# Softmax sums from the exponential's accumulator instead of from products, and the ends of query tiles begun two steps earlier

## The chip, the cores and the metric

The kernel runs on one core of a Trainium2 chip, in one launch. Its engines work beside each other, each on its own queue of instructions: TensorE multiplies matrices (the profile has a row for its products, PE, and one for its weight loads, PEld), VectorE (DVE), ScalarE (ACT) and GpSimd (POOL) do the element-wise work, and SyncE (SP) issues most of the DMAs. The metric is the device time of one execution in microseconds; several runs of a kernel are compared by their medians.

## The reference

Four blocks follow each other on `x` of shape 4 x 512 x 128, all in fp32, each `x = layernorm(x + block(x))`. The change touches the first and, through its order, the second.

```python
# block 1: attention with relative positions, 8 heads of 16
score   = (einsum('bqhd,bkhd->bhqk', q + u_bias, k) + rel_shift(einsum('bqhd,khd->bhqk', q + v_bias, p))) / sqrt(e)
attn    = softmax(score, axis=-1)
ctx     = einsum('bhqk,bkhd->bqhd', attn, v).reshape(b, s, e)
return ctx @ Wo + bo
# block 2: each token goes to one of 8 experts (its largest gate), F = 512
h  = silu(xn @ W1[e] + b1[e]);  ye = h @ W2[e] + b2[e];  out = ye[top1] * top1_score
# block 3: in-projection, causal convolution of 3, gates a, b, c, and the recurrence over 512 positions
state = a_t * state + b_t * u_t;  y_t = c_t * state + u_t
# block 4: each token goes to one of 14 experts, F = 256, gelu
```

## The kernel before

**Attention** is 64 steps (`steps`, L1320): a batch b of 4, a tile t of 128 queries of 4, and a pair p of heads of 4. The loop `attention` (L1331) writes the instructions of each engine out in order, by hand. Step k issues:

- the turning (`flip`, L986) of the probabilities of step k-2: four TensorE transposes of 128x128 into a PSUM bank `ptr`, and a ScalarE copy to `prT`, once before and once after the scores;
- `scores` (L938) of step k: TensorE products into the PSUM tiles `main` and `aux`;
- in every second step `values` (L997), for the two pairs of step k-4 and k-3: 16 products of `prT` with V into `ctx`, and a ScalarE copy into `cT`. V has a column of ones beside each head's 16 columns (L878 to L880), so that `ctx` holds each head's sum of probabilities too;
- `softmax` (L968) of step k: two predicated copies and the row maximum (`nmax`) on VectorE, and one ScalarE exponential of 128x512 per head, into `pr`. The probabilities are not normalized here.

**Side work** goes between these steps: generators in the list `side`, each of which is advanced a little per step. They prepare later batches (`attn_prep`), finish query tiles and batches (`tiles_end`, `attn_end`), route tokens to experts (`route`, `dispatch`), and run the first half of the experts of block 2 (`experts(0, 0, ...)`, batches 0 and 1). All of it shares two PSUM banks (`any`) with `ptr` and `ctx`. A step therefore has a fixed number of places, `room[0]` (L1358): two products' groups of side work, or one if the step also issues a `ctx`. A generator that finds no place left waits for the next step (`bank`, L410). `pause(n)` lets n steps go by.

**The end of a query-tile pair**, `tiles_end` (L1009), runs eight times, for two tiles of one batch each. It takes one place for `pn`: 16 products of 128x4 against `sel` that pick the sums out of `cT`. VectorE inverts them (`rec`), and spreads them (`wide`). A second place goes to `prr` (four transposes of `wide`), after which VectorE multiplies `cT` by it; a third to `po`, the product with the output weights, which VectorE adds to the residual `xs`. The generator is put into `side` when the last `ctx` of its pair has been issued, three steps after the pair's last exponential (L1366). After the second pair of a batch, `attn_end` (L1049) follows: layer norm into `xf`, the transposed `xfT`, then `route` (L523) with its gate product `pl` and the counts of tokens per expert, and `dispatch` (L602) with the product `rank`, which gives every token its place in the sorted rows, and the scatters. Batches are dispatched in two groups, 0 and 1, then 2 and 3 (`GROUPS`). The second batch of a group goes on from the first one's counts.

**After attention**, `play` (L376) interleaves generators by a modelled clock (`Clock`, L63): it takes the first one whose needs are ready at the modelled time, and one that yields `BLOCKED` is passed over for that round. `rest_of_last` (L1641) brings the last query-tile pair (L1647), the last batch's end and routing, and then the experts of batches 2 and 3 (`experts(1, 0, ...)`, whose tokens are transposed into `pxs`). `rest_of_first` (L1631) brings what the first experts have left: up-products `ph`, down-products `py`. Wherever the model expects TensorE to wait more than 2 us for a PSUM bank's first product, it puts products of 128x512 in front whose result nobody reads (`pass_time`, L97, issued at L1666); they are called passes here.

All other instructions are issued by one helper, so that the profile shows them all at its line, L193; they are told apart by tile names.

Of the kernel before, what the change touches and what calls it, by code (L numbers as in the profile page):

```python
# [198 lines left out]
def tile_kernel(ctx: ExitStack, tc: tile.TileContext, x, wpack, cols, rows, tabs, b2bd0, b2bd1,  # L199
# [168 lines left out]
    def done():  # L368

        return clock.last  # L370
# [33 lines left out]
    def pause(n):  # L404

        if now[0] is not None:
            for _ in range(2 * n):
                yield

    def bank(*needs):  # L410
        if psum_e is not None:
            yield (*needs, common_bank)
            return
        while now[0] is not None and not room[0]:
            yield
            yield
        room[0] -= 1
# [101 lines left out]
        return ap.unsqueeze(2).to_broadcast([P, NT, n_e])  # L519

    chosen, before, shares, slots, extra = {}, {}, {}, {}, {}

    def route(xT, weights, n_e, b, layer, out):  # L523

        nm = f"{layer}_{b}"
        gr = GROUP[b]
        at = GROUPS[gr].index(b) * NT
        if at == 0:
            n_t = len(GROUPS[gr]) * NT
            chosen[layer, gr] = plan.tile([P, n_t, n_e], F32, tag=f"chosen{layer}_{gr}", name=f"chosen{nm}")  # L530

            before[layer, gr] = plan.tile([P, n_t + 1, n_e], F32, tag=f"before{layer}_{gr}", name=f"before{nm}")
            nc.gpsimd.memset(before[layer, gr][:, 0, :], 0.0)
        mine = chosen[layer, gr][:, at : at + NT, :]
        w = small.tile([P, NT, 32], F32, tag="w", bufs=5, name=f"w{nm}")
        out.append(w)
        nc.gpsimd.memset(w, 0.0)
        yield from bank(xT)
        lg = ps(f"pl{nm}")[:, : NT * n_e].rearrange("p (n e) -> p n e", e=n_e)
        for n in range(NT):  # L540
            nc.tensor.matmul(lg[:, n, :], lhsT=xT[:, n * P : (n + 1) * P], rhs=weights, start=True, stop=True)
        yield (done(),)
        mx = small.tile([P, NT], F32, tag="mx", name=f"mx{nm}")
        nc.vector.tensor_reduce(mx, lg, AX.X, ALU.max)
        eq = small.tile([P, NT, n_e], F32, tag=f"eq{n_e}", name=f"eq{nm}")
        nc.vector.tensor_tensor(eq, lg, over(mx, n_e), ALU.is_equal)
        ex = small.tile([P, NT, n_e], F32, tag=f"ex{n_e}", name=f"ex{nm}")
        nc.vector.tensor_tensor(ex, lg, over(mx, n_e), ALU.subtract)
        if layer == 0:
            nc.scalar.activation(ex, ex, AF.Exp)  # L550
        else:

            nc.scalar.activation(ex, ex, AF.Tanh, scale=0.5)
        nc.vector.tensor_tensor(eq, eq, ramps[n_e].unsqueeze(1).to_broadcast([P, NT, n_e]), ALU.mult)
        first = small.tile([P, NT], F32, tag="first", name=f"first{nm}")
        nc.vector.tensor_reduce(first, eq, AX.X, ALU.max)
        nc.vector.tensor_tensor(mine, eq, over(first, n_e), ALU.is_equal)
        so_far = before[layer, gr]
        for n in range(at, at + NT):
            nc.vector.tensor_tensor(so_far[:, n + 1, :], so_far[:, n, :], chosen[layer, gr][:, n, :], ALU.add)  # L560
        yield
        yield from pause(1)

        def weighted():
            if layer == 1:
                den = small.tile([P, NT, n_e], F32, tag=f"den{n_e}", name=f"den{nm}")
                nc.vector.tensor_scalar(den, ex, -1.0, 1.0, ALU.mult, ALU.add)
                nc.vector.reciprocal(den, den)
                nc.vector.scalar_tensor_tensor(ex, ex, 1.0, den, ALU.add, ALU.mult)
            sm = small.tile([P, NT], F32, tag="sm", name=f"sm{nm}")  # L570
            nc.vector.tensor_reduce(sm, ex, AX.X, ALU.add)
            share = keep.tile([P, NT], F32, tag=f"share{layer}", name=f"share{nm}")
            nc.vector.reciprocal(share, sm)
            shares[layer, b] = share
            nc.vector.tensor_tensor(w[:, :, :n_e], mine, over(share, n_e), ALU.mult)

        yield from dispatch(b, (xf_of if layer == 0 else x3)[b], n_e, (F0, F1)[layer], ("b1_0", "b1_1")[layer], layer,
                            weighted)
        yield
# [22 lines left out]
    def dispatch(b, its_rows, n_e, n_f, b1, layer, meanwhile):  # L602
# [12 lines left out]
        nov = NOV[gr]  # L615
        mine = slice(i * NT, (i + 1) * NT)
        eq, cum = chosen[layer, gr], before[layer, gr]
        yield from bank(cum, eq)
        both = ps(f"rank{nm}")
        flat, pc = both[:, : NT * n_e], both[:, NT * n_e : (NT + 1) * n_e]  # L620
# [347 lines left out]
    def softmax(b, t, p, main, aux):  # L968

        nm = f"{b}_{t}_{p}"  # L970
        c0 = t * P
        wd = min(P, S - c0 - 1)
        nc.vector.copy_predicated(main[:, :, c0 : c0 + P], low.bitcast(U32).unsqueeze(1).to_broadcast([P, 2, P]),
                                  aux[:, :, 0, :])
        nc.vector.copy_predicated(main[:, :, c0 + 1 : c0 + 1 + wd],
                                  ident[:, :wd].bitcast(U32).unsqueeze(1).to_broadcast([P, 2, wd]), aux[:, :, 1, :wd])
        nmax = small.tile([P, 2], F32, tag="nmax", name=f"nmax{nm}")
        nc.vector.tensor_reduce(nmax, main, AX.X, ALU.max, negate=True)
        prs = []
        for i in range(2):  # L980
            pr = ap6.tile([P, S], F32, tag="pr", name=f"pr{nm}_{i}")
            nc.scalar.activation(pr, main[:, i, :], AF.Exp, bias=nmax[:, i : i + 1])
            prs.append(pr)
        return prs

# [6 lines left out]
        nc.scalar.copy(prT.rearrange("p c q -> p (c q)"), ptr)  # L992
        return prT

    cTs = {}

    def values(b, t, g, prTs):  # L997

# [10 lines left out]
    def tiles_end(b, t2):  # L1009

        nm = f"{b}_{t2}"
        cT = cTs.pop((b, t2))
        yield from bank(cT)
        pn = ps(f"pn{nm}")[:, : 2 * NG * 4]
        for i in range(2):
            for g in range(NG):
                at = (i * NG + g) * 4
                nc.tensor.matmul(pn[:, at : at + 4], lhsT=cT[:, i, g, :], rhs=sel, start=True, stop=True)
        yield (done(),)
        rec = small.tile([P, 2 * NG * 4], F32, tag="rec", bufs=1, name=f"rec{nm}")  # L1020
        nc.vector.reciprocal(rec, pn)
        wide = ap2.tile([P, 2 * NG, 4, 2 * DH], F32, tag="wide", bufs=1, name=f"wide{nm}")
        nc.vector.tensor_copy(wide.rearrange("p g h d -> p (g h) d"), rec.unsqueeze(2).to_broadcast([P, 2 * NG * 4, 2 * DH]))
        yield
        yield from bank(wide)
        pr_ = ps(f"prr{nm}")
        for g in range(2 * NG):
            nc.tensor.transpose(pr_[:, g * P : (g + 1) * P], wide[:, g].rearrange("p h d -> p (h d)"), ident)
        yield (done(),)
        flat = cT.rearrange("p i g q -> p (i g q)")  # L1030
        nc.vector.tensor_tensor(flat, pr_, flat, ALU.mult)
        yield
        yield from bank(cT)
        po = ps(f"po{nm}")
        for i in range(2):
            for g in range(NG):
                nc.tensor.matmul(po[:, i * D : (i + 1) * D], lhsT=cT[:, i, g, :], rhs=wwo[:, g, :],
                                 start=(g == 0), stop=(g == NG - 1))
        yield (done(),)
        mine = xs[b][:, 2 * t2 : 2 * t2 + 2, :].rearrange("p n d -> p (n d)")  # L1040
        nc.vector.tensor_tensor(mine, po[:, : 2 * D], mine, ALU.add)
        if t2 == 1 and b < B - 1:
            gen = attn_end(b)
            side.insert(0, gen)
            if b == GROUPS[0][-1]:
                urgent.append(gen)
        yield
# [283 lines left out]
    def attention(first, last):  # L1331

        for k in range(first, last):
# [29 lines left out]
            for gen in halves:  # L1363
                if gen in side and next(gen, "end") == "end":
                    side.remove(gen)
            if due is not None and due[2] == 1 and due[1] % 2 == 1:  # L1366
                side.insert(int(side[:1] == urgent), tiles_end(due[0], due[1] // 2))

    def wide_ps(name):
        if psum_e is None:  # L1370
# [273 lines left out]
    def rest_of_last():  # L1644
        last_experts = experts(1, 0, pack[0], E0, F0, "b1_0", col("rms_w"))
        next(last_experts)
        yield from tiles_end(B - 1, 1)  # L1647
        yield from attn_end(B - 1)
        yield from last_experts
        load_layer1()  # L1650
        while 1 not in gxs:
            yield BLOCKED
        backs = []
        for b in GROUPS[1]:
            yield (made[0, 1], lambda: clock.free["gpsimd"])
            backs.append(gather(b, 0))
        for b, back in zip(GROUPS[1], backs):
            yield from layer0_end(b, back)
        for b in GROUPS[1]:
            while b - 2 not in over_with:  # L1660
                yield BLOCKED
            begin(recurrence(b), -1)
        yield from layer1(1)
# [114 lines left out]
```

## Time and profile before

| | |
|---|---|
| runs | 579.96, 582.27, 586.38 us; median 582.27 |
| the profiled execution's own time | 601.35 us |
| its span, from first to last instruction | 599.4 us |
| mean granted TensorE clock | 0.888 |
| preparation, before the steps of attention | 0 to 17 us |
| attention with its side work | 17 to 331 us; TensorE busy 280.5, ScalarE 171.0, VectorE 204.3 |
| the last batch's way to its experts | 331 to 374 us; TensorE busy 35.6 |
| second half of block 2's experts | 374 to 410 us; TensorE busy 31.8 of 36 |
| block 3, the recurrences | 410 to 497 us; TensorE busy 82.6 of 87 |
| block 4 | 497 to 599.4 us; TensorE busy 67.3 |

The profile shows one execution, which took 3% longer than the median of the runs. Durations in it are those of that execution. In a row of groups the columns are the line, the engine and the operation, the tile written and the tiles read, the number of instructions, their busy time in us and the mean of one in ns, and behind the bar the idle time of the engine just before them and what ended most of it. In the rows of tenths each digit is a fortieth of the span; PEclk is the clock that was granted to TensorE, as a share of full speed: 9 is full, 5 is half.

### The profile page before, as it was taken

The page shows a single profiled execution, that of the slowest core. Times are in us where ns is not written, and L with a number is a line of the kernel's source. Part 1 is how long each engine was busy: PE and PEld are TensorE (multiplying, and loading weights), DVE is VectorE, ACT ScalarE, POOL GpSimd, SP SyncE. Part 2 cuts the span into 40 slices and gives each one's busy share as a digit, 9 for nine tenths or more (in the row PEclk, how much of TensorE's full clock was granted, in tenths as well). Part 3 has the DMA queues.
Part 4 walks back from the last instruction along what each step waited for, and adds up shares of the span by engine and source line. Part 5 has one row for each costly group of instructions (what it writes and reads, how often), then busy time and mean ns, then how long its engine had stood idle before and what let it go on. Part 6 is the DMA issues. An engine that isn't in the chain of part 4 may idle for free.

```text
span 599.4 us, 11301 instructions
## 1 busy us (share of the span) xinstructions
PE 512.4 (85%) x4132; PEld 362.6 (60%) x4132; DVE 374.4 (62%) x1033; ACT 293.3 (49%) x619; POOL 168.0 (28%) x272
## 2 busy tenths in 40 slices
PE   8988999979689898889898896899989988888740
PEld 6455665756446675567777693796455445876730
DVE  3786776755556746567766664596686689661415
ACT  1256565663546543456665130255546445655541
POOL 2482150230610400202200242522731304143324
PEclk9999999985879957579999787899979979998785
DMA  8998550410000560200118634862100006247321
GB/s 308 333 325 234 135 98 19 82 45 1 19 1 2 89 211 1 72 15 1 71 38 282 212 104 146 302 194 66 35 1 1 18 1 170 85 117 205 104 74 57
DMA packets 63847, 64.03 MB, mean 107 GB/s; under 512 B 4784, under 2 KB 53296, under 8 KB 63536
## 3 DMA queue, kind: packets, MB, share of 16 engines
q1 hardware_dynamic: 61744, 59.12, 33.3%
q0 software_dynamic: 2048, 4.20, 2.2%
q8 instruction: 32, 0.52, 0.4%
q14 instruction: 23, 0.19, 0.1%
HBM read 44.16 MB, written 20.45 MB: 108 GB/s over the span
## 4 chain that ended last, share of the span: by engine, by line
PE 60%; DVE 20%; issue 7%; ACT 6%; DMA 3%; POOL 2%; SPq 0%; DVEq 0%; ACTq 0%; POOLq 0%
PE ptr L193 9%; PE main L193 7%; PE py L193 7%; PE pa L193 6%; PE ph L193 6%; DVE nmax L193 6%; PE ctx L193 5%; DVE main L193 5%; PE aux L193 4%; PE pj L193 3%; DVE hb L193 2%; ACT pr L193 2%; PE pqa L193 1%; PE pxs L193 1%; PE pl L193 1%
## 5 line engine op out<-in xcount | busy, mean ns | idle before, releaser
L193 PE MATMUL ptr<-ident,pr 128*128 128x128 f32 x512 | 91.0, 306 | 22.0 <-ACT prT L193 6.2
L193 ACT COPY prT<-ptr 128x512 f32<-128x512 f32 x128 | 74.5, 587 | 65.3 <-PE ptr L193 63.6
L193 ACT ACTIVATE pr<-main,nmax 128x512 f32<-128x512 f32 x128 | 81.3, 687 | 49.0 <-DVE nmax L193 46.2
L193 PEld LDWEIGHTS ptr<-ident,pr 128*128 128x128 f32 x512 | 61.3, 153 | 66.0 <-issue 15.6
L193 DVE TENSOR_REDUCE nmax<-main 128x2 f32<-128x1024 f32 x64 | 78.4, 1224 | 2.2
L193 DVE COPY_PREDICATED main<-low,aux 128x256 f32<-128x256 uint32 x64 | 27.3, 427 | 80.4 <-PE aux L193 75.2
L193 POOL DMA_INDIRECT back<-made,at x32 | 33.6, 1051 | 48.6 <-DMA made<-ys 30.3
L193 PE MATMUL aux<-Ko,QLo 32*128 32x128 f32 x472 | 46.7, 320 | 0.0
L193 PE MATMUL ctx<-prT,V 128*32 128x128 f32 x1024 | 41.0, 310 | 4.8 <-ACT prT L193 4.4
L193 PE MATMUL main<-KR,QR 32*128 32x512 f32 (+3 forms) x192 | 44.1, 538 | 0.0
L193 PE MATMUL ph<-xt,wd 128*128 128x128 f32 x296 | 41.9, 285 | 2.5 <-DMA wd<-pack 1.2
L193 PE MATMUL py<-wd,hb 128*128 128x128 f32 x248 | 35.4, 295 | 6.9 <-DVE hb L193 5.2
L193 PEld LDWEIGHTS ph<-xt,wd 128*128 128x128 f32 x296 | 37.5, 197 | 6.0 <-issue 1.7
L193 PEld LDWEIGHTS py<-wd,hb 128*128 128x128 f32 x248 | 32.9, 208 | 10.6 <-DVE hb L193 6.3
L193 PEld LDWEIGHTS ctx<-prT,V 128*32 128x32 f32 x1024 | 30.4, 124 | 12.6 <-ACT prT L193 7.4
L193 PEld LDWEIGHTS aux<-Ko,QLo 32*128 32x128 f32 x472 | 34.7, 205 | 0.7 <-DVE QL L193 0.7
L193 ACT ACTIVATE th<-hb 128x512 f32<-128x512 f32 x30 | 18.9, 631 | 32.5 <-DVE hb L193 23.7
L193 ACT ACTIVATE ys<-py 128x128 f32<-128x128 f32 (+1 forms) x65 | 18.9, 294 | 28.6 <-PE py L193 19.9
L193 PE MATMUL main<-K,QL 32*128 32x128 f32 (+2 forms) x192 | 32.4, 416 | 0.0
L193 POOL DMA_INDIRECT sent<-xf,at x16 | 16.7, 1042 | 55.6 <-DVE at L193 39.9
L193 POOL TENSOR_TENSOR QL<-QL,t 128x512 f32<-128x512 f32 x8 | 10.1, 1268 | 73.0 <-DVE t L193 73.0
L193 POOL DMA_INDIRECT sent<-x,at x16 | 17.2, 1072 | 46.3 <-ACT gV L193 20.2
(309 smaller groups left out, 998.7 us busy)
## 6 DMA issues: line engine op xcount, KB each, us to landing
wd<-pack SPq DMA_DIRECT2D x24, 512.0 KB
wd<-pack SPq DMA_DIRECT2D x20, 256.0 KB
pack<-in_W_dram SPq DMA_DIRECT2D x16, 256.0 KB
rows<-sent SPq DMA_DIRECT2D x16, 256.0 KB
made<-ys SPq DMA_DIRECT2D x16, 256.0 KB
pack<-in_W_dram SPq DMA_DIRECT2D x28, 128.0 KB
sent<-zero SPq DMA_DIRECT2D x2, 1344.0 KB
tab<-in_tabs_dram SPq DMA_DIRECT2D x2, 1280.0 KB
```

What stands on the lines that cost most here:

```text
L193: return inner(*args, **kw)
```

## The change

1. Each exponential writes the sum of its row as well (`accum_out`), into one column of a small tile `sums`, of which there is one per query-tile pair.
2. `tiles_end` takes the reciprocal of that tile. The 16 products of `pn`, and the place in PSUM that they took, go. It then lets two steps go by before it takes `cT` up.
3. `tiles_end` is put into `side` at the end of the step that issues the pair's last exponential, where before it was put there when the pair's last `ctx` was issued. The last pair's end is therefore in `side` when attention is over, and `rest_of_last` takes it from there.
4. After attention, `route` of the second batch of a group holds until the first one's counts have been issued, and `dispatch` until the first one's slots are known.

The column of ones in V stays, and so do the sums in `ctx`.

```diff
@@ route
     chosen, before, shares, slots, extra = {}, {}, {}, {}, {}
+    counted = set()
...
         nc.gpsimd.memset(w, 0.0)
+        while at and psum_e is not None and (layer, b - 1) not in counted:
+            yield BLOCKED
         yield from bank(xT)
...
             nc.vector.tensor_tensor(so_far[:, n + 1, :], so_far[:, n, :], chosen[layer, gr][:, n, :], ALU.add)
+        counted.add((layer, b))
@@ dispatch
+        while i and psum_e is not None and (layer, gr) not in further:
+            yield BLOCKED
         yield from bank(cum, eq)
@@ softmax
+        if t % 2 == 0 and p == 0:
+            sums[b, t // 2] = small.tile([P, 2, H], F32, tag="sums", bufs=2, name=f"sums{nm}")
         prs = []
         for i in range(2):
             pr = ap6.tile([P, S], F32, tag="pr", name=f"pr{nm}_{i}")
-            nc.scalar.activation(pr, main[:, i, :], AF.Exp, bias=nmax[:, i : i + 1])
+            nc.scalar.activation(pr, main[:, i, :], AF.Exp, bias=nmax[:, i : i + 1],
+                                 accum_out=sums[b, t // 2][:, t % 2, 2 * p + i : 2 * p + i + 1])
@@ tiles_end
-        cT = cTs.pop((b, t2))
-        yield from bank(cT)
-        pn = ps(f"pn{nm}")[:, : 2 * NG * 4]
-        for i in range(2):
-            for g in range(NG):
-                at = (i * NG + g) * 4
-                nc.tensor.matmul(pn[:, at : at + 4], lhsT=cT[:, i, g, :], rhs=sel, start=True, stop=True)
-        yield (done(),)
         rec = small.tile([P, 2 * NG * 4], F32, tag="rec", bufs=1, name=f"rec{nm}")
-        nc.vector.reciprocal(rec, pn)
+        nc.vector.reciprocal(rec, sums.pop((b, t2)).rearrange("p i h -> p (i h)"))
         wide = ...
-        yield
+        yield from pause(2)
+        cT = cTs.pop((b, t2))
         yield from bank(wide)
@@ attention
-            if due is not None and due[2] == 1 and due[1] % 2 == 1:
-                side.insert(int(side[:1] == urgent), tiles_end(due[0], due[1] // 2))
+            if k < len(steps) and steps[k][1] % 2 == 1 and steps[k][2] == H // 2 - 1:
+                side.insert(int(side[:1] == urgent), tiles_end(steps[k][0], steps[k][1] // 2))
@@ rest_of_last
-        yield from tiles_end(B - 1, 1)
+        for gen in side:
+            if gen.__name__ == "tiles_end":
+                yield from gen
```

More of the change, by code (lines that the diff above doesn't have):

```diff
@@ L993, in flip @@
         return prT
-    cTs = {}
+    cTs, sums = {}, {}
     def values(b, t, g, prTs):
```

## The prediction

> **What bounds the kernel now.** I read the page's slices first, then the groups, the sums' own products (tile pn) by stretch, the timeline around TensorE's waits for ScalarE, and the handover out of attention. On the page, TensorE is the busiest engine and ScalarE half idle. PEclk drops between slices 9 and 18, inside attention (about 17 to 331 us of a 599.4 us span).
>
> ```profile
> PE 512.4 (85%) x4132; PEld 362.6 (60%) x4132; DVE 374.4 (62%) x1033; ACT 293.3 (49%) x619; POOL 168.0 (28%) x272
> ...
> PE   8988999979689898889898896899989988888740
> ...
> PEclk9999999985879957579999787899979979998785
> ```
>
> The groups show what one attention step costs ScalarE: two exponentials and two copies of turned probabilities.
>
> ```profile
> L193 ACT COPY prT<-ptr 128x512 f32<-128x512 f32 x128 | 74.5, 587 | 65.3 <-PE ptr L193 63.6
> L193 ACT ACTIVATE pr<-main,nmax 128x512 f32<-128x512 f32 x128 | 81.3, 687 | 49.0 <-DVE nmax L193 46.2
> ```
>
> Over many steps the copies idle until TensorE has turned the next tile, so ScalarE has room there. The timeline shows where it has none: at 121.89 the copies follow the exponentials without a gap, and TensorE waits 1.44 us for them; at 285.96 it waits 1.22 us for xt, which stood behind two exponentials. ex, at 141.00, is the smallest kind of ScalarE instruction in this program.
>
> ```profile
> 120.73 1.27 ACT L193 ACTIVATE pr<-main,nmax 128x512 f32<-128x512 f32 x2 [1.05 <-DVE nmax L193]
> ...
> 121.89 1.07 ACT L193 COPY prT<-ptr 128x512 f32<-128x512 f32 x2
> 122.53 1.08 PE L193 MATMUL ctx<-prT,V 128*32 128x128 f32 x32 [1.44 <-ACT prT L193]
> ...
> 141.00 0.23 ACT L193 ACTIVATE ex<-ex 128x32 f32<-128x32 f32 x1
> ...
> 285.21 0.69 ACT L193 ACTIVATE xt<-pxs,colt 128x512 f32<-128x512 f32 x1
> 285.96 0.66 PE L193 MATMUL ptr<-ident,pr 128*128 128x128 f32 x4 [1.22 <-ACT xt L193]
> ```
>
> **Part by part.** The sums are made against the profiled execution, 601.35 us: the span of 599.4 and 1.95 around it. It is 19.1 us above the runs' median of 582.27. The clock rows below explain most of that, I think; the differences are carried to the median.
>
> *Products removed.* The busy time of pn, cut by tile end (first column: the stretch; then its length, PE busy, PEld, DVE, clock):
>
> ```profile
> 101.00:104.00 3.00, 0.95 (x8) 0.97 (x8) 0.00 (x0) 1.00 0.00 0
> 139.00:142.00 3.00, 1.87 (x8) 1.78 (x8) 0.25 (x1) 0.50 0.00 0
> ...
> sum 22.00, PE 10.09 PEld 9.82 DVE 1.05; mean PE 1.26 PEld 1.23 DVE 0.13
> ```
>
> Eight ends cost 10.1 us of TensorE, 0.95 each at full clock, 1.87 at half. The last lies behind attention; the seven inside are 10.1 - 0.95 = 9.1 us. TensorE sets the pace there: **-9.1**. The wait of pn for its PSUM bank (2.6 us on prT) isn't saved: the next product takes the same two banks.
>
> *Places refilled.* Each step has a fixed number of side places. By the changed program's order, the freed ones move everything up; at the last ctx of attention two ph and two py more have been issued (ph 10 and 11, py 3 and 4). They come out of the stretch behind attention, but cost TensorE here: 2 x 1.16 (a ph at 318) + 2 x 2.0 (py at 320, 331): **+6.3**.
>
> *Sums added.* The program still lists one instruction per exponential, and no row of before has an accumulator output. Below: nothing. Above: a whole further ScalarE instruction of ex's 0.23. Two exponentials take 1.27, not 2 x 0.687 = 1.37, so neighbours overlap by 0.10; I take 0.23 - 0.10 = 0.13 each, 0.26 a step, nearest to the ex row. It would be hidden wherever the second copy of prT idles longer. I count 21 of 64 steps with less cover than 0.26 or with TensorE waiting for the ScalarE row behind the exponentials (the steps at 33 and 44 us, and most of those from 120 to 130, 200 to 206, at 261 and from 280 to 322): 21 x 0.26 = **+5.5**. Uncovered everywhere it is 64 x 0.26 = 16.6, at the upper price 29.4; at zero price 0. Here a rule speaks against the change: the Trainium skill, VectorE: DVE Perf Modes, section Two Vector instructions with no wait between them, says that an operation which writes out its accumulator is two instructions, the second a read. It is stated for VectorE, and no run here has shown it. Carried over it gives the 5.5; not carried over, 0. I keep the 5.5.
>
> *Clock.* The next two rows: in 122 to 130 TensorE was busy 5.56 of 8 us; then the clock was 0.5 for 15 us. (Columns: stretch, length, PE, PEld, DVE, ACT, POOL busy, clock, DMA.)
>
> ```profile
> 122.00:130.00 8.00, 5.56 (x80) 3.94 (x80) 4.83 (x10) 5.46 (x11) 2.85 (x7) 1.00 0.06 13
> 131.00:146.00 15.00, 14.27 (x116) 10.56 (x112) 6.48 (x19) 5.76 (x11) 0.00 (x0) 0.50 0.01 2
> ```
>
> Between 120 and 272 us there are five such falls, some 71 us in all. A step at half clock takes 6.6 us (ptr at 134.34 to ptr at 140.95), one at full clock 4.2 (100.10 to 104.31), so they cost about 71 x (1 - 4.2/6.6) = 26 us, 5.2 each. By the Trainium skill, TensorE: Matmul & The Clock Gate, section Part 1: The HAM clock gate, the clock falls after an idle window of about 3.4 us; the longest wait of TensorE in these steps is 2.74 us (xnT at 162.6), and falls follow waits of 0.7 to 1.5. By the rule the longer ScalarE runs cost no clock, 0; by the rows each may cost 5.2. The moved steps may also close one: I take half a fall, **+2.6**, from -5.2 to +10.4.
>
> *Ends moved.* rec and wide come two steps ahead of prr, on data that the last exponential left; on DVE they stand behind the next nmax, about 3 us after that exponential, so their new wait on ScalarE is free. If it weren't, the hb and mask copies behind them would wait. The ends issue no DMA. On POOL, the second sum into QL and the memsets of QR and V now stand behind var, rstd and x of the batch that ended (0.83 + 1.67 + 4 x 0.20 + 3.92 at 280.8 to 288.6, some 7 us), for a batch that begins a dozen steps of 4.2 us later: 0. The new holds (counted, further) put no instruction in a queue: they keep the planner from issuing batch 3's routing before batch 2's counts. The rest is the handover after attention's last ctx (ends 330.93):
>
> ```profile
> 334.79 0.63 PE L193 MATMUL prr<-ident,wide 128*128 128x128 f32 x4 [0.41 <-DVE wide L193]
> ...
> 349.47 0.96 PE L193 MATMUL pl<-colt,xfT 128*128 128x8 f32 x8
> ...
> 356.06 0.29 PE L193 MATMUL rank<-before,ones 128*128 128x8 f32 x2
> ```
>
> This is batch 3's way to its scatters, which the next experts' tokens (pxs at 373.26) wait for. In the new order prr follows ctx at once (at 334.79 it stood behind py 3 and pn), 3.8 us earlier. pl no longer stands behind a ph (xfT is done at 347.65, pl starts at 349.47: 1.8), nor rank behind ph 13 and py 5 (the counts are done at 352.36, rank starts at 356.06: 3.7). Back comes 1.3: on POOL the memset of batch 2's counts now stands behind batch 3's rstd (1.66 us), and DVE's sums wait for it, xf after them. On SP the last two results of the first experts now go out behind rows 1_0, but that is earlier too, and the weights of blocks 11 and 12 go ahead of the second experts' loads. 3.8 + 1.8 + 3.7 - 1.3: **-8.0**.
>
> *Keep-alive passes.* The recording layer puts 512-column products where it expects TensorE idle. In the new order 5 stand in the recurrences (before one pgx, one pb, three before pa_3_0), where before had none and TensorE was busy 82.6 of 87 us (410 to 497). Two took 1.88 us at 360.4, so 5 x 0.94 = **+4.7**, or idle time of that length: either way it comes off the 8.0. Three passes less in the last experts lay in waits: 0.
>
> Sum: -9.1 + 6.3 + 5.5 + 2.6 - 8.0 + 4.7 = +2.0; profiled 603.4, median **584.3 us**. Without reads and falls the sum is -6.1; with both at their upper ends, 29.4 and 10.4, the time is 616, with reads free and one fall less 571.
>
> **Rivals.**
> *A, no price on ScalarE.* The accumulator comes free, and no fall is added: 2.0 - 5.5 - 2.6 = -6.1, **576.2**; with one fall less, 571. For it: ScalarE is idle half the time, and the copies wait 63.6 us on ptr. Against: 21 steps without cover.
> *B, ScalarE becomes the pace of attention.* Each read costs 0.23 unoverlapped, in half of the steps (32 x 0.46 = 14.7), and the wider waits bring one more fall (5.2): -6.1 + 14.7 + 5.2 = +13.8, **596**. Its place is the step whose first prT copy follows the exponentials at once. It decides once reads and falls together pass 11.9 us: from -6.1 that is +5.8, or +1%.
> *C, the change doesn't shorten the ends.* pn goes, but the next bank user waits as long, and the handover is paced by weights or scatters: -8.0 falls away, **592**.
>
> **How the numbers follow.** Chances: the forecast 0.40 (576.5 to 588), A 0.18, B 0.28, C 0.14. C and B are both slower. A range of 572 to 599 leaves out the far ends of A and B. Within 1% (about what a measurement of this kernel tells from no change) is 576.4 to 588.1: 0.40; faster 0.18; slower 0.42.
>
> **What would show it.** Right: no pn; some 128 more ScalarE rows of 0.1 to 0.3 us, or a longer exponential; attention's last ctx within 5 us of before at like clock; about 34 us from it to pxs of the second experts instead of 42.3. Wrong if: TensorE's waits for prT grow past 10 us in attention (B); the handover still takes 42 us (C); or the exponential stays at 687 ns with nothing behind it (A). How many half-clock stretches a run happens to have can hide all of this.

## The result, and the profile after

The changed kernel is slower. Its median is 599.46 us against 581.12 for the kernel before, a ratio of 1.032 [1.023, 1.041]. On another chip the ratio was 1.015 [1.009, 1.022]. The forecast was 584.3, with a range of 572 to 599. Chips differ by about 2% here (medians of the kernel before: 581, 586, 595 and 586 us), so every ratio below is to the kernel before on the same chip. A ratio compares only those runs of each kernel that lie within 1.5% of its fastest.

The execution of before that is shown ahead of the prediction had an unusual share of half clock (601.35 us against a median of 582). For the comparison the kernel before was profiled once more (582.88 us, span 581.2).

From the page of the changed kernel: the first counts, and the slices of TensorE and of its clock.

```profile
PE 496.3 (83%) x4076; PEld 350.2 (59%) x4076; DVE 378.5 (63%) x1033; ACT 303.5 (51%) x747; POOL 170.1 (29%) x272
...
PE   8997997977789888788999779889998969895930
...
PEclk9878999987979867899999978999998998897985
```

TensorE has 56 rows fewer (4132 before): the 64 of pn are gone, and passes have 28 instead of 20. An end's pn is four products (two tiles of two groups, `NG` = 2), which the profile lists as 8 rows; the 16 of the sections above is the number of its columns. ScalarE has 128 rows more (619 before). The clock looks no worse than before.

The next two fences cut each span at the same four events: the end of attention's last ctx, the first pxs of the second experts, the first pgx (the recurrences begin), and the last pgo. Columns: the stretch, its length, busy time of TensorE, weight loads, VectorE, ScalarE and GpSimd, granted clock, DMA. First the kernel before, in its second profile:

```profile
17.00:325.30 308.30, 273.99 (x2930) 189.87 (x2928) 205.24 (x430) 170.53 (x314) 73.27 (x159) 0.92 0.36 101
325.30:364.60 39.30, 29.58 (x186) 23.16 (x186) 25.52 (x106) 7.09 (x18) 13.54 (x14) 0.96 0.46 153
364.60:385.80 21.20, 18.48 (x159) 17.88 (x160) 15.67 (x41) 8.51 (x18) 10.51 (x9) 1.00 0.89 294
385.80:498.00 112.20, 105.19 (x401) 60.64 (x400) 83.96 (x262) 60.15 (x116) 35.70 (x41) 0.94 0.19 54
498.00:581.20 83.20, 53.55 (x409) 49.10 (x408) 37.59 (x170) 43.10 (x152) 29.56 (x32) 0.85 0.39 115
```

The changed kernel:

```profile
17.00:340.40 323.40, 275.94 (x2920) 192.52 (x2921) 209.74 (x436) 183.40 (x446) 73.43 (x158) 0.91 0.35 100
340.40:373.90 33.50, 27.89 (x135) 20.30 (x135) 22.29 (x100) 5.23 (x13) 13.68 (x16) 0.85 0.39 127
373.90:399.60 25.70, 22.04 (x191) 21.47 (x192) 17.90 (x45) 10.62 (x23) 10.12 (x9) 1.00 0.90 285
399.60:514.20 114.60, 104.53 (x379) 58.74 (x378) 85.16 (x268) 59.80 (x115) 39.16 (x43) 0.96 0.18 51
514.20:596.90 82.70, 51.59 (x403) 47.90 (x402) 36.16 (x162) 41.92 (x149) 29.65 (x30) 0.83 0.38 108
```

Attention is 15.1 us longer, the handover 5.8 shorter, the second experts 4.5 longer, the recurrences 2.4 longer, and the rest 0.5 shorter: together 15.7, the difference of the spans. So the loss is in attention. TensorE's busy time there grew by 2.0 us only; its idle time grew from 34.3 to 47.5. The changed kernel's TensorE waits in attention, longest first (who waited for whom: total, times, longest) have two rows that before does not have at all, K and Ko:

```profile
PE ptr L193 <- ACT prT L193: 12.6, 14, 2.1
PE ctx L193 <- ACT prT L193: 6.8, 10, 0.7
PE ptr L193 <- DVE K L193: 4.8, 2, 2.4
PE ptr L193 <- ACT xt L193: 3.6, 4, 1.4
PE aux L193 <- DMA Ko<-K: 2.8, 1, 2.8
```

In the second profile of before the same view begins so:

```profile
PE ptr L193 <- ACT prT L193: 8.8, 12, 2.1
PE ptr L193 <- ACT xnT L193: 4.9, 3, 2.7
PE ctx L193 <- ACT prT L193: 4.4, 5, 1.4
```

One of the two waits on K, from the changed kernel's timeline (start, length, engine, operation, and in brackets the idle time before it with what ended it):

```profile
119.30 1.02 PE L193 MATMUL pk<-xnT,wp 128*128 128x512 f32 x2
119.96 1.22 DVE L193 TENSOR_REDUCE nmax<-main 128x2 f32<-128x1024 f32 x1
120.20 0.66 PE L193 MATMUL ptr<-ident,pr 128*128 128x128 f32 x4
...
121.51 1.26 POOL L193 TENSOR_TENSOR QL<-QL,t 128x512 f32<-128x512 f32 x1
121.59 2.11 DVE L193 TENSOR_SCALAR xf<-xs,mv_b,rstd_b 128x128 f32<-128x128 f32 x4 [0.41 <-POOL rstd_b L193]
123.55 0.74 DVE L193 SCALAR_TENSOR_TENSOR K<-pk,colt,tab 128x512 f32<-128x512 f32 x1
124.34 0.66 PE L193 MATMUL ptr<-ident,pr 128*128 128x128 f32 x4 [2.42 <-DVE K L193]
124.92 1.19 PE L193 MATMUL ctx<-prT,V 128*32 128x128 f32 x32
126.04 2.08 PE L193 MATMUL pv<-wp,xnT 128*128 128x128 f32 x8
```

`pk`, the next batch's key product, sits in one of the two shared PSUM banks until VectorE has read it into K. On VectorE that read now stands behind xf, the norm of the batch that has just ended. The norm waits 0.41 us for its standard deviation and takes 2.11; K's read ends at 124.29, and only then can the next ptr have the bank. Right behind it pv runs at half clock (2.08 us instead of 1.16). Before, xf stood behind K in both places.

Why is xf there? The ends of tiles begin earlier and have one place less to wait for, so the batch's end (`attn_end`), which follows the second one, begins two steps earlier too. This is theory O, that the new order of the side work is the loss. Its rival was theory R, the accumulator reads on ScalarE.

### The profile page after: what moved, and what is told of

The parts are those of the page before. It is cut to its first block, busy times and chain, and to the rows that moved or that the text cites. A ratio compares the mean times of both kernels' runs of the same rounds, so it can differ in the third digit from the quotient of the medians.

```text
span 596.9 us, 11316 instructions
## 1 busy us (share of the span) xinstructions
PE 496.3 (83%) x4076; PEld 350.2 (59%) x4076; DVE 378.5 (63%) x1033; ACT 303.5 (51%) x747; POOL 170.1 (29%) x272
## 3 DMA queue, kind: packets, MB, share of 16 engines
q1 hardware_dynamic: 61744, 59.12, 33.5%
## 5 line engine op out<-in xcount | busy, mean ns | idle before, releaser
L193 PE MATMUL ptr<-ident,pr 128*128 128x128 f32 x512 | 88.9, 301 | 31.2 <-ACT prT L193 12.6
L193 ACT ACTIVATE pr<-main,nmax 128x512 f32<-128x512 f32 x128 | 87.0, 685 | 49.7 <-DVE nmax L193 48.5
L193 PE MATMUL aux<-Ko,QLo 32*128 32x128 f32 x472 | 44.4, 307 | 2.8 <-DMA Ko<-K 2.8
L193 PE MATMUL main<-KR,QR 32*128 32x512 f32 (+3 forms) x192 | 41.1, 497 | 0.3 <-DMA KR<-K 0.3
L193 POOL DMA_INDIRECT sent<-xf,at x16 | 16.5, 1034 | 81.7 <-DVE at L193 38.1
L193 PEld LDWEIGHTS aux<-Ko,QLo 32*128 32x128 f32 x472 | 32.8, 195 | 3.6 <-issue 3.6
L193 PE MATMUL py<-wd,hb 128*128 128x128 f32 x248 | 32.8, 281 | 0.2
L193 PEld LDWEIGHTS py<-wd,hb 128*128 128x128 f32 x248 | 30.7, 197 | 2.4 <-issue 1.2
L193 PE MATMUL main<-K,QL 32*128 32x128 f32 (+2 forms) x192 | 30.6, 396 | 0.0
L193 DVE COPY_PREDICATED main<-ident,aux 128x256 f32<-128x256 uint32 (+1 forms) x64 | 27.4, 428 | 2.2
L193 POOL DMA_INDIRECT sent<-x,at x16 | 17.6, 1101 | 34.3 <-issue 11.5
L193 DVE SCALAR_TENSOR_TENSOR res<-back,share,res 128x128 f32<-128x128 f32 x16 | 5.7, 358 | 33.3 <-DMA back<-made,at 33.1
```

The lines of the kernel that those rows point to most:

```text
L193: return inner(*args, **kw)
```

## The experiments

**The kernel before again.**

> The kernel before, unchanged, for a profile whose clock is like that of the changed kernel's. Ratio 1.00 within 0.01, 578 to 587 us. Both theories need it only as the other side of the comparison by steps: in the profiles at hand the 64 steps of attention end 8 us later in the changed kernel although that of before shows more half-clock time, so by this profile the steps of the changed kernel should end some 15 us later.

Measured: 1.002 [0.998, 1.005]. It gave the profile that stands above. At step 16 the changed kernel's profile is 1.5 us later than this one, at step 32 12.6, and at the last step, 63, 13.6. Nearly all of the loss thus comes between steps 16 and 32, in which batch 0 is finished and batch 2 prepared. Steps 32 to 63, with the second wait on K (step 37), add only 1.0 net; the kernel before has a stretch of half clock there too (207 to 228 us).

**The reads alone, in the kernel before.**

```diff
-            nc.scalar.activation(pr, main[:, i, :], AF.Exp, bias=nmax[:, i : i + 1])
+            nc.scalar.activation(pr, main[:, i, :], AF.Exp, bias=nmax[:, i : i + 1],
+                                 accum_out=sums[b, t // 2][:, t % 2, 2 * p + i : 2 * p + i + 1])
```

> The kernel before, in which the exponentials also write their sums, into a tile that nobody reads; pn, all places and the order stay. Theory R (the accumulator reads on ScalarE make attention longer): most of the 18 us, 592 to 600 us. Theory O (the new order of the side work makes it longer: batches prepared later or at worse places): 0 to +5 us, 580 to 586. By the profile two exponentials with their reads take 0.18 us more than without, which is 11.5 us if none of 64 steps hides it.

Measured: 1.010 [1.003, 1.017], which is 5.9 us of the median of 582.27 (1.7 to 10.1). That is a third of a loss of 3.2%, two thirds of one of 1.5, and lies between the theories. The price is seen in ScalarE's timeline. The second profile of the changed kernel (from the chip with 1.015), in a step without gaps:

```profile
129.61 0.69 ACT L193 ACTIVATE pr<-main,nmax 128x512 f32<-128x512 f32 x1 [1.13 <-DVE nmax L193]
130.19 0.19 ACT L193 ACTIVATION_READ_ACCUMULATOR pr<-main,nmax 128x1 f32 x1
130.29 0.68 ACT L193 ACTIVATE pr<-main,nmax 128x512 f32<-128x512 f32 x1
130.86 0.20 ACT L193 ACTIVATION_READ_ACCUMULATOR pr<-main,nmax 128x1 f32 x1
130.95 0.58 ACT L193 COPY prT<-ptr 128x512 f32<-128x512 f32 x1
```

The kernel before, likewise:

```profile
125.28 1.27 ACT L193 ACTIVATE pr<-main,nmax 128x512 f32<-128x512 f32 x2 [1.05 <-DVE nmax L193]
126.44 1.07 ACT L193 COPY prT<-ptr 128x512 f32<-128x512 f32 x2
```

From the first exponential to the copy behind the second it is 1.34 us, before 1.16: 0.18 for two reads of 0.2, as they overlap their neighbours.

**The changed kernel without the reads.**

```diff
-        nc.vector.reciprocal(rec, sums.pop((b, t2)).rearrange("p i h -> p (i h)"))
+        nc.vector.reciprocal(rec, ones[:, : 2 * NG * 4])
```

with the exponentials of before.

> The changed kernel without the accumulator output; the reciprocal is taken of a constant tile of ones, so the normalization of the probabilities is left out. Order and places are those of the changed kernel. Theory R: the loss goes, 578 to 585 us. Theory O: it stays, 592 to 600 us.

Measured: 1.035 [1.027, 1.042]. The loss stays, so theory R falls: the reads are not what makes the changed kernel slower. TensorE still waits 4.6 us for K in this run. That the reads cost nothing in the changed kernel isn't shown: it did not run on this chip, and attention has a lower clock in this profile (0.87; 0.91 in the changed kernel's).

**Sums from the exponentials, pn's place kept empty, all else as before.**

```diff
         yield from bank(cT)
-        pn = ps(f"pn{nm}")[:, : 2 * NG * 4]
-        ... its products
         yield (done(),)
-        nc.vector.reciprocal(rec, pn)
+        nc.vector.reciprocal(rec, sums.pop((b, t2)).rearrange("p i h -> p (i h)"))
```

with the exponentials of the changed kernel.

> The kernel before with the sums from the exponentials and without the 16 products of pn, but pn's place in the step stays taken (and empty), and the end of a tile pair begins where it began before. So neither the early ends nor the refilled places are in it. Theory R: 585 to 595 us, the reads less up to 9 us for pn. Theory O: 574 to 582 us, faster than before by the products that went.

Measured: 1.038 [1.030, 1.046], against both. But attention ends at 327.5 us, 2.2 after the kernel before; the loss lies behind it. From this run, the handover and the recurrences (39.3 and 112.2 us long before):

```profile
327.50:379.90 52.40, 40.38 (x196) 28.17 (x192) 29.81 (x120) 7.71 (x18) 21.99 (x23) 0.84 0.40 131
...
386.20:529.50 143.30, 132.17 (x580) 80.43 (x579) 99.82 (x300) 70.70 (x144) 38.54 (x46) 0.98 0.25 73
```

Without the last end's products the planner orders everything behind attention differently. So the time of this run says nothing about attention's part; the next two keep the order behind attention.

**The same, with the last end's pn left in**, so that the order behind attention stays that of before.

> The kernel before with sums from the exponentials and no pn in the seven ends inside attention, their place kept empty; the last end keeps its pn products, so that the order behind attention stays that of before. This is the clean price of reads less products: by the steps of the run with places kept, a step that lost its pn is 0.9 us shorter and the next one 0.4 to 1.3 longer, so 7 products bring 2 us, not 9; the reads cost 3 to 6. Ratio 1.00 to 1.01. If the products were worth their full 9 us: 0.99 to 0.995.

Measured: 0.997 [0.993, 1.001], between the two expectations. Against the reads alone (1.010, on another chip) it is 1.35 points less, with an uncertainty of 0.8, which would make the seven pn worth 7.9 us (3 to 13). But this doesn't settle their price. Over all 22 runs the median is 599.35 against 595.03, a ratio of 1.007, and the reads alone have 1.007 over all of theirs. In the two profiles, steps 0 to 40, in which four of the seven pn went, differ by 1 us, and steps 40 to 48 by 8.6; there the reads alone have 24 us at half clock, and this kernel 3.

**The changed kernel with the old order inside attention.**

```diff
-        yield from pause(2)
+        if (b, t2) == (B - 1, 1):
+            yield from pause(2)
+        else:
+            yield from pause(3)
+            yield from bank()     # pn's place, empty
+            yield
+            yield
         cT = cTs.pop((b, t2))
```

> The changed kernel, but in the seven ends inside attention the place of pn stays taken, and empty, and prr comes in its old step: TensorE's order in attention is that of before without pn, and what is left of the change is the reads, the earlier rec and wide, the last end and the holds behind attention. Theory O (the new order of the side work inside attention is the loss): attention ends within 3 us of before, the handover stays at about 35 us, and the ratio to before is 0.985 to 1.005. If the loss were in the holds or in the order behind attention: 1.02 to 1.035.

Measured: 0.999 [0.995, 1.002]. Attention ends at 326.0 us (325.3 before), and the handover takes 34.5 us from the start of the last ctx (40.4 before, 34.6 in the changed kernel). The changed order inside attention is the loss, and not what comes behind it.

**The freed place alone**: the seven ends begin in their old step again.

```diff
-            if k < len(steps) and steps[k][1] % 2 == 1 and steps[k][2] == H // 2 - 1:
-                side.insert(int(side[:1] == urgent), tiles_end(steps[k][0], steps[k][1] // 2))
+            if due is not None and due[2] == 1 and due[1] % 2 == 1 and due[:2] != (B - 1, NT - 1):
+                side.insert(int(side[:1] == urgent), tiles_end(due[0], due[1] // 2))
+            if k == len(steps) - 1:
+                side.insert(int(side[:1] == urgent), tiles_end(B - 1, 1))
```

and `pause(1)` in `tiles_end` for these seven.

> The changed kernel, but the seven ends inside attention begin where they began before (prr and po in their old steps); only the place of pn is free for what comes next. The last end is that of the changed kernel. If the freed place does it (preparation moved up by one): 1.02 to 1.035. If the early ends do it (the norm of the finished batch comes two steps earlier and meets the next batch's keys on VectorE): 0.99 to 1.01.

Measured: 0.994 [0.992, 0.997]. So preparation that moves up by a place doesn't cost by itself; the loss needs the ends to begin early. On VectorE xf stands behind K and V here.

**The norm two steps later**, all other parts of the change as they are.

```diff
+        yield from pause(2)
         xf = keep2.tile([P, NT, D], F32, tag="xf", ...)
```

> The changed kernel, but the end of a batch lets two steps go by ahead of its norm xf, so that on VectorE xf stands behind the reads of pk and pv again and no longer ahead of K. If that meeting is the main loss, TensorE's waits of 2.4 us on K (steps 21 and 37) and the long step behind each go, some 3 us a batch with a clock fall less: ratio 1.015 to 1.025, attention 6 to 9 us shorter than in the changed kernel. If the meeting is only one of many: 1.025 to 1.035.

Measured: 0.990 [0.987, 0.994]. This goes further than I expected: one line turns a loss of 1.5 to 3% into a gain of 1%. Once more, beside the changed kernel on one chip:

> The changed kernel with the norm xf two steps later, once more, beside the changed kernel: ratio to before 0.985 to 0.998, 3.5 to 4.5% under the changed kernel.

> The changed kernel itself, on the chip of the runs beside it: ratio to before 1.025 to 1.04 again.

Measured: 0.989 [0.985, 0.993], and the changed kernel 1.015 [1.009, 1.022], 2.6% apart, less than the 4.2% of the first pair. By this profile attention is about as long as before (the last ctx ends at 324.1 us; 325.3 before), and the gain lies mostly in the handover (33.2 us instead of 39.3). The same place in the timeline of the kernel with the later norm:

```profile
116.64 1.02 PE L193 MATMUL pk<-xnT,wp 128*128 128x512 f32 x2
117.30 1.22 DVE L193 TENSOR_REDUCE nmax<-main 128x2 f32<-128x1024 f32 x1
118.44 0.74 DVE L193 SCALAR_TENSOR_TENSOR K<-pk,colt,tab 128x512 f32<-128x512 f32 x1
119.23 0.66 PE L193 MATMUL ptr<-ident,pr 128*128 128x128 f32 x4
120.59 1.08 PE L193 MATMUL ctx<-prT,V 128*32 128x128 f32 x32 [0.70 <-ACT prT L193]
121.60 1.16 PE L193 MATMUL pv<-wp,xnT 128*128 128x128 f32 x8
```

K is read as soon as nmax is done, ptr does not wait, and pv runs at full clock.

**The norm's VectorE time put back**: the norm runs at its early place too, and what follows it stays late.

```diff
+        if now[0] is not None:
+            apply_norm(xf, xs[b], mean, both, nc.vector)
+        yield from pause(2)
         apply_norm(xf, xs[b], mean, both, nc.vector)
```

> The kernel with the norm two steps later, with one thing added: xf's four instructions (2.11 us of VectorE a batch, three batches) are issued at their early place too, and their result is written over two steps later. All that follows the norm (pxf, pl, rank) stays late. If it is VectorE's time ahead of K that costs: back up to 1.015 to 1.03. If it is the order of what follows the norm (pxf beside pv, the gates, the ranks): 0.99 to 1.00.

Measured: 1.009 [1.006, 1.012], 2.0% above the kernel with the later norm. That is less than the 1.015 I wrote down, but most of the way: twelve VectorE instructions whose result nobody reads cost 2%. Eight of them stand where the next batch is prepared. The timeline shows a wait back in both places, on K in the first, and in the second on t, the read of another such product (pqb):

```profile
122.83 2.41 DVE L193 TENSOR_SCALAR xf<-xs,mv_b,rstd_b 128x128 f32<-128x128 f32 x4 [0.42 <-POOL rstd_b L193]
125.17 0.74 DVE L193 SCALAR_TENSOR_TENSOR K<-pk,colt,tab 128x512 f32<-128x512 f32 x1
...
125.96 0.79 PE L193 MATMUL ptr<-ident,pr 128*128 128x128 f32 x4 [2.81 <-DVE K L193]
126.68 1.94 PE L193 MATMUL ctx<-prT,V 128*32 128x128 f32 x32
...
204.99 1.11 DVE L193 TENSOR_SCALAR xf<-xs,mv_b,rstd_b 128x128 f32<-128x128 f32 x4 [0.43 <-POOL rstd_b L193]
206.82 0.66 PE L193 MATMUL ptr<-ident,pr 128*128 128x128 f32 x4 [2.12 <-DVE t L193]
```

**The norm one step later**: behind K, ahead of V. The edit is `pause(1)` in place of `pause(2)`.

> The changed kernel with xf one step later, not two: on VectorE it then stands behind K, and ahead of V's additions, which empty the bank of pv. If it is the place ahead of K that costs: 0.99 to 1.00. If any place ahead of a read of the two banks costs the same: 1.015 to 1.03.

Measured: 1.010 [1.006, 1.014], between the two expectations. Its timeline has no wait on K, and none on V, so neither expectation had the reason:

```profile
120.40 0.74 DVE L193 SCALAR_TENSOR_TENSOR K<-pk,colt,tab 128x512 f32<-128x512 f32 x1
...
123.44 1.18 DVE L193 TENSOR_SCALAR xf<-xs,mv_b,rstd_b 128x128 f32<-128x128 f32 x4
124.75 0.89 DVE L193 TENSOR_TENSOR V<-pv,rowt 128x128 f32<-128x128 f32 x4
...
126.64 0.60 PE L193 MATMUL pxf<-ident,xf 128*128 128x128 f32 x4
...
130.59 0.66 PE L193 MATMUL ptr<-ident,pr 128*128 128x128 f32 x4 [1.33 <-ACT prT L193]
131.97 1.94 PE L193 MATMUL ctx<-prT,V 128*32 128x128 f32 x32 [0.73 <-ACT prT L193]
```

What is early here is pxf: it starts 3.1 us behind the start of pv, in the changed kernel 4.5, with the norm two steps later 8.0. Four us after pxf TensorE waits 1.33 and 0.73 us for prT, and then it runs at half clock: 132 to 148 us was granted 0.50. Both profiles of the changed kernel have the same two waits at the same step, with a slow ctx behind them (1.91 and 1.93 us). With the norm two steps later there is one wait of 1.70 us near this place, and 128 to 144 us was granted 1.00; a fall comes there only later (154 to 174 us at 0.50). So an early norm costs by a second way, what follows it. That the fall of the clock comes from these waits is argued from where it stands; no run separates the two.

The two ways stand apart when the steps are summed. In the table, "meeting" is the length of steps 20 to 23 and 36 to 39, in which the norm meets K, and "behind" that of steps 24 to 27 and 40 to 43, from the row maximum of each stretch's first step to that of the step after it; all lengths are in us, from one profile each.

| kernel | xf stands | ratio to before | last ctx ends | meeting | behind |
|---|---|---|---|---|---|
| before, again | behind K | 1.002 | 325.3 | 32.6 | 40.0 |
| changed | ahead of K | 1.032; 1.015 | 340.4; 334.5 | 37.0; 35.4 | 47.8; 46.5 |
| changed, norm one later | ahead of V | 1.010 | 335.8 | 30.5 | 50.9 |
| changed, norm two later | behind V | 0.990; 0.989 | 327.4; 324.1 | 31.4; 31.4 | 34.0; 34.0 |
| the same, norm run at both places | ahead of K (result unused) | 1.009 | 345.3 | 38.1 | 37.1 |
| changed, ends in their old step | behind V | 0.994 | 318.4 | 31.8 | 33.6 |

In these profiles the norm's VectorE time costs in the meeting (38.1 against 31.4), and what follows the norm costs more, behind it (50.9 against 34.0): there the changed kernel has 24 and 20 us at half clock, the norm one later 38, the norm two later none. But the kernel before has 20 us there as well, so the clock isn't all of it; why these steps are longer in the changed kernel stays open. The profile of the norm at both places is of its longest run (595.67 us; median 589.04), so its 345.3 overstates its loss.

## Why the prediction was wrong, step by step

**Attention.** The prediction's sum inside attention was -9.1 + 6.3 + 5.5 + 2.6 = +5.3 us; measured +15.1. Behind attention it had -8.0 + 4.7 = -3.3; measured +0.6. The miss is 9.8 and 3.9 us.

- *Products removed, -9.1.* Not settled. The one estimate is 7.9 us (3 to 13), and it is gone when all runs are taken. The profiles show 1 us over the steps in which four of the seven went; most of their further difference lies where one has 24 us at half clock and the other 3.
- *Places refilled, +6.3.* The place itself did no harm (0.994 with the place free, 0.999 with it kept). Its price in TensorE's time was not measured alone.
- *Ends moved, 0 inside attention.* This step failed. It followed rec, wide, hb and the mask copies on VectorE, and stopped there at the tile's end. But the batch's end moves with it. On POOL the prediction saw this (var, rstd and x ahead of QL, put at 0); on VectorE it did not ask whom that batch's xf would stand in front of. It moved from behind K to ahead of it, and pxf came earlier too. With xf and what follows it two steps later, the same kernel is at 0.99; of the 2.6% that this brings on one chip, the norm's VectorE time alone takes back 2.0.
- *On POOL and SP, 0.* Too low: the DMA into Ko came late for step 17, and TensorE waited 2.8 us. The kernel with the later norm has this wait too (2.8 and 2.9), so it isn't what decided.
- *Sums added, +5.5.* Right in mechanism, and the size partly by luck: alone they cost 5.9 us (1.7 to 10.1). A read is 0.2 us long as an instruction and costs 0.09 net, not 0.13; 64 steps of 0.18 are 11.5, and half of that shows, where the prediction counted a third of the steps at 0.26.
- *Clock, +2.6.* About right in size in the first profile: 0.92 of 308.3 us is 49 us at half clock before, 0.91 of 323.4 us is 58 after, and 9 us at half clock cost 9 x (1 - 4.2/6.6) = 3.3. In the second profile of the changed kernel it is 44 us (0.93 of 317.6), less than before, and attention is still 9 us longer. So a worse clock alone doesn't make the loss.
- *Handover, -8.0.* Right in kind: from ctx's end to pxs 33.5 us, as forecast ("about 34"), but the kernel before needs 39.3 in its second profile, not 42.3. The term measures -5.8, at unlike clock: 0.85 in the changed kernel's handover, 0.96 in that of before.
- *Passes, +4.7.* Five stand in the recurrences, as forecast, and take 4.9 us of TensorE; that stretch is 2.4 us longer. The experts ahead of it are 4.5 longer and have no passes. What makes them longer was not tried.

**The rivals.** B named nearly the right time (596) for the wrong reason: TensorE's waits for prT did grow, from 13.2 to 19.4 us, but they were 17.5 without the reads, at the same loss, and 17.7 with the later norm, which gains. Its sign, over 10 us, could tell nothing, as the kernel before was already past it. A and C fell: the reads have a price, and the handover did become shorter.

Of the prediction's signs of being right, attention's last ctx within 5 us of before at like clock is the one that failed.

## What to carry to other kernels

When a change lets a chain of side work begin earlier, follow the whole chain to its end, and for each of its instructions ask what it now stands in front of on its engine, and who waits for that. Here a norm of 2.1 us ahead of the read that empties a PSUM bank made TensorE wait 2.4 us, though VectorE is idle a third of the time in attention; and what followed the norm cost as well. And a change that loses may be one wrong place: a gain of 1% lay under a loss of 1.5 to 3%, and one line of delay uncovered it.

## What the runs showed of the hardware

The accumulator output of an exponential is a second ScalarE instruction of 198 ns, in all 128 cases:

```profile
L193 ACT ACTIVATION_READ_ACCUMULATOR pr<-main,nmax 128x1 f32 x128 | 25.4, 198 | 0.0
```

It starts 0.1 us before the exponential ends, and the next instruction 0.1 us before it ends, so it costs 0.09.

The norm ahead of K took 2.11 us, and 1.11 where it stood two steps later. In the changed kernel its first quarter took 1.27 us, against a usual 0.34, and ended 0.1 us after GpSimd's addition into QL (1.26 us, from 121.51), which had started 0.08 earlier. The Trainium skill, SBUF — State Buffer, section SBUF: two separate sides, says that VectorE and GpSimd share a pair of ports as an exclusive lock for a whole instruction. This row agrees; the next quarters don't show it, as they took 0.34 to 0.41 beside GpSimd's own norm x. So about 0.9 us of the 2.42 us wait (1.27 less 0.34, an estimate) is this meeting of VectorE and GpSimd. In the kernel with the norm at both places, the early norm of the second place had no addition into QL beside it, and took 1.11 us.
